# Graph attention over gathered rows: scores one block in front of the products in two layers, TensorE's second waits left out, late ring places freed by the group

## The chip, the cores and the metric

The kernel runs on one core of one Trainium2 chip. The metric is the device time of one execution in microseconds (us). The program uses five engines: TensorE (PE; its weight loads are PEld), VectorE (DVE), ScalarE (ACT), GpSimd (POOL) and SyncE (SP, which only issues DMAs here).

## What is computed

The input is `x`, 4096 nodes of 256 float32 features, and `adj`, a 4096 x 4096 int32 adjacency matrix with about 8 neighbours a row. Four graph-attention layers follow each other; each adds to `x` what it makes of the normalised rows:

```python
h = jnp.maximum(_layernorm(x, axis=-1), 0.0)
x = x + _L0_gnn_ref(h, adj, L0_gnn_W, L0_gnn_a)      # 4 heads, leaky_relu .2, softmax over neighbours, elu
...
x = x + _L1_gnn_ref(h, adj, L1_gnn_W, L1_gnn_a)      # 1 head, leaky_relu .01, h@W + att @ node
...
x = x + _L2_gnn_ref(adj, h, L2_gnn_weights, L2_gnn_biases, L2_gnn_phis)   # 4 heads, leaky_relu .2
...
x = x + _L3_gnn_ref(h, adj, L3_gnn_Wq, ...)          # 4 heads, scores q.k / 8, softmax over neighbours
```

In each layer a node's new row is a weighted sum of its neighbours' rows; the weights are a softmax over the node's neighbours. The four layers are called l=0 to l=3 below; the change's "layers two and three" are l=1 and l=2.

## The kernel before

**Lists in place of the matrix.** The function `scan` reads `adj` in 128 loads of 512 KB, turns each row into a list of neighbours, and while it reads already fetches the first six neighbours of every node for l=0 (tiles `s_g`, line L1030 of GpSimd, sums on TensorE at L630). The nodes are then put in order of their degree. `late` does the rest of l=0: 93 more fetches, in groups of up to two blocks of 128 nodes (`LATE`), into a large tile `s_ring`, products at L1237, and the rows for l=1 are scattered to a table in device memory (L1047).

**A layer.** `layer(1)`, `layer(2)` and `layer(3)` each work through 32 blocks of 128 nodes in the order 0, 30, 1, 29, ..., 17, 14, 16, 15, 31 (`ORDER`). A block has as many ring slots as its highest degree (most have 8 or 9, block 31 has 3). For each block the steps are:

- *fetch* (`fill`, L1030): GpSimd fetches one slot's 128 rows from the layer's table with an indirect DMA. The ring `s_ring` has 64 slots in l=1, 69 in l=2 and fewer, wider ones in l=3; a fetch into a used slot waits until the block that had it is done.
- *score* (`scores`): `s_e` from the fetched rows, on ScalarE in l=1 (L1507, L1508, exp at L1550, beside a check of the lists at L1564 and L1568 on VectorE), on VectorE in l=2 (L1510 to L1553, exp on ScalarE at L1556).
- *weights* (`weigh`): sum and reciprocal (L1582, L1583), shares (L1584), the node's own row (L1595, `s_me`), then VectorE scales the fetched rows in place (L1610) and TensorE sums them by products with an identity matrix: `x` itself (L1590), the scaled rows (L1617), the own row (L1623), all into `s_acc`.
- *settle* (`settle`, `normed`): VectorE reduces `s_acc` into `x` (L1644) and takes mean and variance (L955, L957); ScalarE works out scale and shift (`s_y`, L960 to L967); one step later it makes the normalised row `s_h` (L970).
- *norm* and *flip* (`turned`): TensorE transposes `s_h` (L980), ScalarE copies it out as `s_ht` (L982).
- *product* (`advance`, `times`, L1019 the bias, L1023 the weights) and *third*: the next layer's row. In l=1 it is one product of 264 columns, copied out (L1663 or L1665) and written by SP to the table of l=2 (L1667). In l=2 it is a product of 512 columns (k and v) and one of 256 (q), copied out at L1683 and L1687, multiplied and reduced (L1690, L1694), squared on ScalarE (L1697), and written by SP to the table of l=3 (L1685).

**What sets the order.** In l=1 and l=2 the order of instructions on PE, DVE, ACT and SP is the one in which the program issues them, and the loop of `layer` is written for that. For block number i of the order it fetches ahead (`fill(i)`, up to four blocks), then runs norm and product of older blocks, score and weights of block i, then settle, flip and third of older blocks. How far each stage lags behind is set by the five numbers S, N, F, Q, T, which shrink over the last blocks:

```python
S = 1 if left < 5 else 2
N = 2 if left < 4 else 3
Q = 2 if left < 2 else 3 if left < 4 else 4 if left < 6 else 5
F, T = max(N, Q - 1), Q + 1
...
p = self.scores(l, b, self.rows[b], g)
...
sums[b] = self.weigh(l, b, vs.pop(b) if l == 3 else self.rows[b][:, 0:D], g, p)
```

A layer's fetches can begin only when the table that the layer before writes is complete.

Of the kernel before, what the change touches and what calls it, by code (L numbers as in the profile page):

```python
# [75 lines left out]
AHEAD = 4  # L76

# [3 lines left out]
class Sparse:  # L81
# [500 lines left out]
    def early(self, j):  # L582


        nc, pool = self.nc, self.pool
        E, H = EARLY, 4
        two = self.keep[:, 2 * j : 2 * j + 2, :]
        g = pool.tile([P, 2, E, W], F32, name=f"s_g_{j}", tag="g", bufs=4)
        for u in range(2):
            for k in range(E):  # L590
                self.fetched = self.in_turn(
                    self.fetch(g[:, u, k, :], self.tab[0], self.ids[:, 2 * j + u, k : k + 1])
                )
        yield
        most, src, tot = (two[:, :, 2 * D + k * H : 2 * D + (k + 1) * H] for k in range(3))
        e = pool.tile([P, 2, E + 1, H], F32, name=f"s_ee_{j}", tag="ee", bufs=2)
        nc.vector.tensor_tensor(e[:, :, E, :], most, src, ALU.add)
        nc.vector.tensor_tensor(
            e[:, :, :E, :], g[:, :, :, D : D + H],
            src.unsqueeze(2).to_broadcast([P, 2, E, H]), ALU.add,  # L600
        )
        nc.vector.scalar_tensor_tensor(e, e, 0.2, e, ALU.mult, ALU.max)
        by_head = e.rearrange("p u k h -> p u h k")
        nc.vector.tensor_reduce(most, by_head, AX.X, ALU.max)
        nc.vector.tensor_tensor(
            by_head, by_head, most.unsqueeze(3).to_broadcast([P, 2, H, E + 1]), ALU.subtract
        )
        p = self.pe.tile([P, 2, E + 1, H], F32, name=f"s_pe_{j}", tag="p", bufs=1)
        nc.scalar.activation(p, e, AF.Exp)
        yield  # L610
        nc.vector.tensor_reduce(tot, p.rearrange("p u k h -> p u h k"), AX.X, ALU.add)
        me = pool.tile([P, 2, D], F32, name=f"s_mee_{j}", tag="mee", bufs=2)
        nc.vector.tensor_tensor(
            me.rearrange("p u (h d) -> p u h d", h=H),
            two[:, :, D : 2 * D].rearrange("p u (h d) -> p u h d", h=H),
            p[:, :, E, :].unsqueeze(3).to_broadcast([P, 2, H, D // H]), ALU.mult,
        )
        for u in range(2):
            yield
            v = g[:, u, :, 0:D].rearrange("p k (h d) -> p k h d", h=H)  # L620
            nc.vector.tensor_tensor(  # L621
                v, v, p[:, u, 0:E, :].unsqueeze(3).to_broadcast([P, E, H, D // H]), ALU.mult
            )
        yield
        acc = self.pp.tile([P, IB], F32, name=f"s_ae_{j}", tag="ps")
        acc = acc.rearrange("p (u d) -> p u d", u=2)
        nc.tensor.matmul(acc, lhsT=self.ident, rhs=me, start=True, stop=False)
        yield
        for k in range(E):
            nc.tensor.matmul(  # L630
                acc, lhsT=self.ident, rhs=g[:, :, k, 0:D], start=False, stop=(k == E - 1)
            )
            yield
        nc.scalar.copy(two[:, :, D : 2 * D], acc)
        yield
# [252 lines left out]
    def more_scores(self, l, mine, ge, e):  # L888
# [4 lines left out]
        if l < 3:  # L893
            nc.tensor.matmul(
                ps[:, 0:H], lhsT=self.to_edge, rhs=mine[:, D + H : D + 2 * H], start=True,
                stop=True,
            )
            nc.vector.tensor_tensor(s, ge[:, D : D + H], ps[:, 0:H], ALU.add)
        else:
            nc.tensor.matmul(ps[:, 0:D], lhsT=self.to_edge, rhs=mine[:, 0:D], start=True, stop=True)  # L900
            nc.vector.tensor_tensor(ge[:, 0:D], ge[:, 0:D], ps[:, 0:D], ALU.mult)
            nc.vector.tensor_reduce(
                s, ge[:, 0:D].rearrange("p (h d) -> p h d", h=H), AX.X, ALU.add
            )
# [9 lines left out]
        self.give(self.got)  # L914
# [12 lines left out]
        self.give(self.got)  # L927

    def more_rows(self, l, p, ge):
# [12 lines left out]
        self.give(self.got)  # L942
# [3 lines left out]
        nc.vector.tensor_tensor(v, v, s.unsqueeze(2).to_broadcast([P, H, D // H]), ALU.mult)  # L946
# [4 lines left out]
    def normed(self, pool, xt, name):  # L951
# [7 lines left out]
        log, root, less, minus, r, at = (y[:, k : k + 1] for k in range(6))  # L959
        act(log, mv[:, 1:2], AF.Ln, bias=self.eps)  # L960
# [8 lines left out]
        h = pool.tile([P, D], F32, name=f"s_h_{name}", tag="h", bufs=2)  # L969
# [3 lines left out]
    def turned(self, pool, h, name):  # L973
        nc = self.nc
        ht = pool.tile([P, KC, P], F32, name=f"s_ht_{name}", tag="ht", bufs=3)
        pt = self.bank(f"s_pht_{name}")
        self.wrote, k = [], self.groups is not None and self.got
        self.spot = pt[:, KC * P :], k
        for c in range(KC):
            self.writes(nc.tensor.transpose(pt[:, ts(c, P)], h[:, ts(c, P)], self.ident))  # L980
        yield None
        self.read_by = nc.scalar.copy(  # L982
            ht, pt[:, : KC * P].rearrange("p (c r) -> p c r", c=KC)
        ).ins
        self.give(k)
        yield ht

    def bank(self, name):
# [5 lines left out]
        self.got = k  # L994
# [20 lines left out]
    def times(self, ht, w, width, name, bias=None, ps=None):  # L1015
# [11 lines left out]
        return ps[:, :width]  # L1027

# [28 lines left out]
    def layers(self):  # L1057
        tc, nc, nt = self.tc, self.nc, self.nt
        with ExitStack() as ctx:
# [19 lines left out]
            self.past, self.took_x, self.seen = [], {}, []  # L1079
# [23 lines left out]
    def late(self):  # L1103
# [5 lines left out]
        todo, held, at = list(range(len(LATE))), {}, 0  # L1109
# [34 lines left out]
        def fill(i):  # L1144
            nonlocal at
            deliver()
            while todo and todo[0] <= i + 4:
# [4 lines left out]
                j = todo.pop(0)  # L1152
                for u, b in enumerate(LATE[j]):
                    for k in range(K):
                        last[j] = take(
                            ring[:, s + u * K + k, :], self.tab[0],
                            self.near[:, b, EARLY + k : EARLY + k + 1],
                        )
                last.setdefault(j, last.get(j - 1))
# [36 lines left out]
        def weigh(i):  # L1196
# [29 lines left out]
            g = gathered(i)  # L1226
            for u in range(m):
                for k0 in range(0, K, AT_ONCE):
                    k1 = min(k0 + AT_ONCE, K)
                    v = by_heads(g[:, u, k0:k1, 0:D])  # L1230
                    nc.vector.tensor_tensor(
# [3 lines left out]
                    )  # L1235
            for k in range(K):
                nc.tensor.matmul(  # L1237
                    acc, lhsT=self.ident, rhs=g[:, :, k, 0:D], start=False, stop=(k + 1 == K)
                )
            sums[i] = acc  # L1240

# [68 lines left out]
    def layer(self, l):  # L1310
# [8 lines left out]
        past = self.past  # L1319
# [9 lines left out]
        def fill(i):  # L1329
            nonlocal at  # L1330
            while todo and nt - len(todo) <= i + AHEAD:
# [20 lines left out]
                for k in range(K):  # L1352
                    at_k = self.near[:, j, k : k + 1]
                    g = self.fetch(ring[:, s + k, :], self.tab[l], at_k).ins
                    next_in_line(g)
                    if k == 0:
# [8 lines left out]
                    for some, _ in ends:  # L1365
                        for m in some:
                            self.tc.declare_no_dep(g, m, reason="its block's last is waited for")
# [9 lines left out]
                if more:  # L1377
                    next_in_line(self.fetch(ring[:, s + KEPT, :], self.tab[l], self.far).ins)
                held[j] = (s, s + room)
                at = s + room if K else at  # L1380

        sums, behind, turning, flipped, rows = {}, {}, {}, {}, {}
# [18 lines left out]

        def room(k):
# [4 lines left out]
        def norm(d):  # L1407
            if l < 3:
                room(1)
                turning[d] = self.turned(self.pool, next(behind.pop(d)), f"{l + 1}_{d}")  # L1410
                next(turning[d])
                when["turn", d] = now, self.wrote
# [33 lines left out]
        stages = {"settle": settle, "norm": norm, "flip": flip, "product": product, "third": third}  # L1446
# [6 lines left out]

        for i in range(nt):
            now = i
            left = nt - 1 - i
            if l == 3:
                S = 1 if left < 3 else 2
                N = F = Q = S + 1
                T = N  # L1460
            else:
                S = 1 if left < 5 else 2
                N = 2 if left < 4 else 3
                Q = 2 if left < 2 else 3 if left < 4 else 4 if left < 6 else 5
                F, T = max(N, Q - 1), Q + 1
# [4 lines left out]
            upto("norm", i - N)  # L1470
            upto("product", i - Q)
            g = ring[:, held[b][0] : held[b][1], :]
            p = self.scores(l, b, self.rows[b], g)
            if l == 3:
                upto("third", i - T)
            sums[b] = self.weigh(l, b, vs.pop(b) if l == 3 else self.rows[b][:, 0:D], g, p)
            start, end = held.pop(b)
            past.append((start * wide, end * wide, self.read))
            if l < 3:
                signals[i] = self.read[1]  # L1480
            upto("settle", i - S)
            if l < 3:
                upto("flip", i - F)
                upto("third", i - T)
# [4 lines left out]
        upto("settle", nt - 1)  # L1489
        upto("norm", nt - 1)  # L1490
# [4 lines left out]
    def scores(self, l, b, mine, g):  # L1495
# [29 lines left out]
        else:  # L1525
# [3 lines left out]
            for k0 in range(0, G, AT_ONCE):  # L1529
                m = min(AT_ONCE, G - k0)  # L1530
                kq = g[:, k0 : k0 + m, 0:D]
                nc.vector.tensor_tensor(  # L1532
                    kq, kq, q.unsqueeze(1).to_broadcast([P, m, D]), ALU.mult
                )
                nc.vector.tensor_reduce(  # L1535
# [10 lines left out]
        p = self.shares[:, ts(self.turns % 2, TOPK * H)].rearrange("p (k h) -> p k h", h=H)  # L1546
        if l == 1:
# [23 lines left out]
    def weigh(self, l, b, me, g, made):  # L1571
# [15 lines left out]
        self.turns += 1  # L1587
# [11 lines left out]
        if more:  # L1599
            rows = self.more_rows(l, p, g[:, KEPT, :])  # L1600
            some.append(
                nc.tensor.matmul(
                    acc[:, 0, :], lhsT=self.to_row, rhs=rows, start=False, stop=False
                ).ins
            )
        step = 2 if b in ORDER[-2:] else AT_ONCE
        for k0 in range(0, G, step):
            m = min(step, G - k0)
            v = g[:, k0 : k0 + m, v0 : v0 + D].rearrange("p k (h d) -> p k h d", h=H)
            nc.vector.tensor_tensor(  # L1610
                v, v, p[:, k0 : k0 + m, :].unsqueeze(3).to_broadcast([P, m, H, D // H]), ALU.mult
            )
            k = k0
            while k < k0 + m:
                n = min(2, k0 + m - k) if some else 1
                some.append(
                    nc.tensor.matmul(  # L1617
                        acc[:, 0:n, :], lhsT=self.ident, rhs=g[:, k : k + n, v0 : v0 + D],
                        start=False, stop=False,
                    ).ins  # L1620
# [9 lines left out]
    def settle(self, l, b, acc, made):  # L1630
# [5 lines left out]
        if l == 3:  # L1636
            tag = ("out", "kv")[ORDER.index(b) % 2]
# [12 lines left out]
    def advance(self, l, b, ht, made):  # L1650
# [5 lines left out]
        if l == 2:  # L1656
            short = b in ORDER[-2:]
            ps = self.times(ht, self.we2, W, name, None if short else self.be2)
            of_row = self.got
# [8 lines left out]
        else:  # L1668
            ps = self.times(ht, self.wkv, 2 * D, f"kv{name}")
            of_kv = self.got  # L1670
# [5 lines left out]
            else:  # L1676
                ps_q = self.times(ht, self.wq, D, f"q{name}")
                of_q = self.got
# [597 lines left out]
```

## Time and profile before

| | |
|---|---|
| seven runs, us | 1671.3, 1674.87, 1671.38, 1674.92, 1670.75, 1671.05, 1676.24 |
| median | 1671.38 us |
| the profiled execution | 1675.34 us, of which its span is 1673.6 us |
| mean granted TensorE clock | 0.831 |
| PE busy | 1076.5 us (64%), 3179 instructions |
| PEld busy | 586.0 us (35%) |
| DVE busy | 1109.5 us (66%), 2651 instructions |
| ACT busy | 535.8 us (32%), 1754 instructions |
| POOL busy | 1141.6 us (68%), 1241 instructions |

The profile is of one execution. Times are us from the start of its span. A row of a timeline gives the start, the duration, the engine, the line of the kernel, the operation and the tiles (out <- in), a count where several like instructions follow each other, and in brackets how long the engine was idle before it and what released it. A group gives busy time and mean duration, and then the idle time ahead of its instructions. The stages lie about like this: scan to 350, late 366 to 545, l=1's fetches 545 to 883, l=2's 909 to 1247, l=3's from 1282 on.

### The profile page before, as it was taken

The page shows a single profiled execution, that of the slowest core. Times are in us where ns is not written, and L with a number is a line of the kernel's source. Part 1 is how long each engine was busy: PE and PEld are TensorE (multiplying, and loading weights), DVE is VectorE, ACT ScalarE, POOL GpSimd, SP SyncE. Part 2 cuts the span into 40 slices and gives each one's busy share as a digit, 9 for nine tenths or more (in the row PEclk, how much of TensorE's full clock was granted, in tenths as well). Part 3 has the DMA queues.
Part 4 walks back from the last instruction along what each step waited for, and adds up shares of the span by engine and source line. Part 5 has one row for each costly group of instructions (what it writes and reads, how often), then busy time and mean ns, then how long its engine had stood idle before and what let it go on. Part 6 is the DMA issues. An engine that isn't in the chain of part 4 may idle for free.

```text
span 1673.6 us, 14552 instructions
## 1 busy us (share of the span) xinstructions
PE 1076.5 (64%) x3179; PEld 586.0 (35%) x3179; DVE 1109.5 (66%) x2651; ACT 535.8 (32%) x1754; POOL 1141.6 (68%) x1241
## 2 busy tenths in 40 slices
PE   5858878605776357777775477778794455545465
PEld 4523333203443134444343234444452222322232
DVE  5669899816885254455552456676774797888777
ACT  6966665003344023333343023333342000000000
POOL 1167777767774777777772777777762777777775
PEclk9969989857897578898897689999997677777878
DMA  7899999466552344444452435444542776767674
GB/s 265 287 395 394 359 395 337 140 217 175 154 167 68 110 119 128 131 132 131 132 138 65 109 108 145 137 134 134 146 130 89 209 220 206 215 202 213 202 209 143
DMA packets 125910, 309.11 MB, mean 185 GB/s; under 512 B 35028, under 2 KB 53463, under 8 KB 125816
## 3 DMA queue, kind: packets, MB, share of 16 engines
q0 software_dynamic: 66832, 203.64, 41.7%
q1 hardware_dynamic: 58984, 104.46, 17.6%
q8 instruction: 29, 0.48, 0.1%
q14 instruction: 65, 0.53, 0.1%
HBM read 273.00 MB, written 35.00 MB: 184 GB/s over the span
## 4 chain that ended last, share of the span: by engine, by line
POOL 26%; DMA 23%; DVE 19%; issue 16%; ACT 9%; PE 6%; DVEq 0%; POOLq 0%; SPq 0%; ACTq 0%
POOL s_ring L1030 21%; DMA s_ring<-s_tab,s_near 12%; DMA s_raw<-in_adj_dram 9%; DVE s_ring L1610 5%; ACT s_low L277 2%; POOL s_placed L721 2%; POOL s_g L1030 2%; DVE s_ring L1532 1%; DVE s_e L1535 1%; PE s_acc L1237 1%; PE s_bank L1023 1%; PE s_ps_t L1023 1%; DVE s_rx L1644 1%; DVE s_me L1595 1%; POOL out_dram L1047 1%
## 5 line engine op out<-in xcount | busy, mean ns | idle before, releaser
L1030 POOL DMA_INDIRECT s_ring<-s_tab,s_near x900 | 854.3, 949 | 339.9 <-issue 263.0
L1617 PE MATMUL s_acc<-s_ring,s_ident 128*128 128x512 f32 (+1 forms) x1002 | 454.4, 610 | 278.4 <-DVE s_ring L1610 278.3
L1617 PEld LDWEIGHTS s_acc<-s_ring,s_ident 128*128 128x128 f32 x1002 | 221.1, 228 | 489.8 <-DVE s_ring L1610 309.1
L1030 POOL DMA_INDIRECT s_g<-s_tab,s_keep x192 | 183.2, 954 | 131.6 <-DMA s_raw<-in_adj_dram 67.6
L1610 DVE TENSOR_TENSOR s_ring<-s_ring,s_shares 128x2048 f32<-128x2048 f32 (+1 forms) x153 | 233.0, 1554 | 0.0
L277 ACT ACTIVATE s_low<-s_raw 128x1024 fp8e4<-128x1024 int32 x128 | 135.1, 1055 | 64.1 <-DMA s_raw<-in_adj_dram 62.1
L1556 ACT ACTIVATE s_shares<-s_e 128x40 f32<-128x40 f32 (+7 forms) x64 | 13.1, 205 | 331.6 <-DVE s_e L1553 331.6
L520 PE MATMUL s_pt<-s_low,s_mark_True 128*128 128x512 fp8e4 x256 | 83.6, 407 | 53.6 <-DVE s_cand L532 47.2
L1532 DVE TENSOR_TENSOR s_ring<-s_ring,s_shares 128x2048 f32<-128x2048 f32 (+7 forms) x47 | 78.8, 1676 | 56.2 <-DMA s_ring<-s_tab,s_near 38.2
L960 ACT ACTIVATE s_y<-s_mv,s_eps 128x1 f32<-128x1 f32 x64 | 18.8, 294 | 276.6 <-DVE s_mv L957 250.5
L532 DVE MAX8 s_cand<-s_pt 128x8 f32<-128x256 f32 x256 | 93.4, 420 | 13.8 <-PE s_pt L530 13.8
L1564 DVE TENSOR_SCALAR s_eq<-s_ring,s_own_f 128x207 bf16<-128x207 f32 (+12 forms) x32 | 12.4, 388 | 131.9 <-DMA s_ring<-s_tab,s_near 131.7
L630 PE MATMUL s_ae<-s_g,s_ident 128*128 128x512 f32 x192 | 94.3, 622 | 3.4 <-DVE s_g L621 3.4
L1535 DVE TENSOR_REDUCE s_e<-s_ring 128x32 f32<-128x2048 f32 (+7 forms) x47 | 78.9, 1679 | 1.6
L1023 PE MATMUL s_bank<-s_wkv,s_ht 128*128 128x512 f32 x128 | 66.3, 644 | 3.6 <-ACT s_ht L982 3.6
L1023 PE MATMUL s_ps<-s_we_l,s_ht 128*128 128x264 f32 x128 | 45.9, 514 | 23.9 <-ACT s_ht L1271 23.9
L520 PEld LDWEIGHTS <-s_mark_True 128*128 128x128 bf16 x256 | 23.4, 101 | 105.1 <-issue 54.8
L1590 PE MATMUL s_acc<-s_rx,s_ident 128*128 128x256 f32 x192 | 59.9, 395 | 0.0
L1623 PE MATMUL s_acc<-s_me,s_ident 128*128 128x256 f32 x192 | 57.1, 379 | 0.0
L1268 PE MATMUL s_pht<-s_ident,s_rx 128*128 128x128 f32 x64 | 13.8, 325 | 65.6 <-ACT s_rx L1261 57.9
L621 DVE TENSOR_TENSOR s_g<-s_g,s_pe 128x1536 f32<-128x1536 f32 x32 | 55.5, 1740 | 0.0
L922 PE MATMUL s_bank<-s_to,s_to_row 128*128 128x32 f32 (+1 forms) x6 | 1.8, 394 | 81.1 <-DVE s_to L916 81.1
(286 smaller groups left out, 1842.0 us busy)
## 6 DMA issues: line engine op xcount, KB each, us to landing
s_raw<-in_adj_dram SPq DMA_DIRECT2D x128, 512.0 KB, 9.8
s_ring<-s_tab,s_near POOLq DMA_INDIRECT x900, 3.0
s_rx<-s_placed SPq DMA_DIRECT2D x32, 262.0 KB, 3.8
s_tab<-s_kv SPq DMA_DIRECT2D x32, 256.0 KB, 2.3
s_tab<-s_rx SPq DMA_DIRECT2D x32, 132.0 KB, 2.0
s_keep<-in_x_dram SPq DMA_DIRECT2D x8, 512.0 KB, 9.4
s_vself<-s_tab SPq DMA_DIRECT2D x32, 128.0 KB, 3.4
s_tab<-s_keep SPq DMA_DIRECT2D x7, 528.0 KB, 3.2
```

The source lines that it names most:

```text
L277: nc.scalar.activation(low[r][:, quarter(q)], raw.pop(q), AF.Copy, saturate=False, accum_out=self.sums[:, r, h : h + 1],)
L520: nc.tensor.matmul(pt, lhsT=self.mark[k], rhs=lo[:, k * PAIR + g * IB : k * PAIR + (g + 1) * IB], start=(k == 0), stop=False,)
L532: nc.vector.max(out=cand[:, g * (IB // CH) + k, :], in_=pt[:, ts(k, CH)])
L630: nc.tensor.matmul(acc, lhsT=self.ident, rhs=g[:, :, k, 0:D], start=False, stop=(k == E - 1))
L1023: self.writes(self.nc.tensor.matmul(ps[:, :width], lhsT=ht[:, c, :], rhs=w[:, c, :], start=(c == 0 and bias is None), stop=(c == KC - 1),))
L1030: return self.nc.gpsimd.indirect_dma_start(out=out, out_offset=None, in_=table[:, :], in_offset=bass.IndirectOffsetOnAxis(ap=idx, axis=0),)
L1532: nc.vector.tensor_tensor(kq, kq, q.unsqueeze(1).to_broadcast([P, m, D]), ALU.mult)
L1535: nc.vector.tensor_reduce(e[:, k0 : k0 + m, :], kq.rearrange("p k (h d) -> p k h d", h=4), AX.X, ALU.add)
L1590: self.took_x[b] = nc.tensor.matmul(acc[:, 1, :], lhsT=self.ident, rhs=self.x[b], start=True, stop=False)
L1610: nc.vector.tensor_tensor(v, v, p[:, k0 : k0 + m, :].unsqueeze(3).to_broadcast([P, m, H, D // H]), ALU.mult)
L1617: nc.tensor.matmul(acc[:, 0:n, :], lhsT=self.ident, rhs=g[:, k : k + n, v0 : v0 + D], start=False, stop=False,).ins
L1623: last = nc.tensor.matmul(acc[:, 0, :], lhsT=self.ident, rhs=mev, start=False, stop=True).ins
```

## The change

It has three parts.

1. *TensorE's second waits.* The products that sum fetched rows (L630, L1237, L1617) follow VectorE's scaling of the same rows, which has itself waited for the fetches. A new helper `behind` declares that a product need not wait for the fetches too. A second helper, `covered`, does the same for VectorE's scaling and for fetches against the earlier products on reused ring slots (`ever`).
2. *Late ring places.* In `late`, the first fetch of a group that takes over ring slots waits for the last product of the group that had them; the other rows' own waits for single products are left out.
3. *Scores in front.* In l=1 and l=2, block i+1's score is issued ahead of block i's weights, except for the last two turns (`left` of 1 or 0), the ScalarE part of the norm becomes a stage `curve` of its own, and the lags come from a table `LAGS`. The tile `s_h` has three buffers instead of two, and l=3's output tile takes them over. l=3's loop keeps its order.

The core of the diff:

```diff
+LAGS = [
+    (1, 1, 2, 2, 2), (1, 1, 2, 2, 2), (1, 1, 2, 2, 3), (1, 1, 3, 3, 3), (1, 2, 3, 3, 4),
+    (2, 2, 3, 3, 4), (2, 2, 4, 4, 5), (2, 3, 4, 5, 6),
+]
...
@@ normed
         y = pool.tile([P, 6], F32, name=f"s_y_{name}", tag="y1", bufs=3)
         log, root, less, minus, r, at = (y[:, k : k + 1] for k in range(6))
+        yield None
         act(log, mv[:, 1:2], AF.Ln, bias=self.eps)
...
-        h = pool.tile([P, D], F32, name=f"s_h_{name}", tag="h", bufs=2)
+        h = pool.tile([P, D], F32, name=f"s_h_{name}", tag="h", bufs=3)
...
+    def covered(self, g, start, size):
+
+        for a, b, some in self.ever:
+            if a < start + size and start < b:
+                for o in some:
+                    self.tc.declare_no_dep(g, o, reason="its block's last is waited for")
+
+    def behind(self, got, product):
+
+        for f in got:
+            self.tc.declare_no_dep(product.ins, f, reason="VectorE's products come in between")
+        return product
...
@@ late, fill
+                ends = [e for a, b, e in past if a < high and low < b]
...
+                        if u == k == 0:
+                            for _, end in ends:
+                                self.tc.add_manual_dep(
+                                    g, end.name,
...
+                                    reason="the group's slots are free",
+                                )
+                        self.covered(g, (s + u * K + k) * W, W)
...
@@ layer
+        def curve(c):
+            if l < 3:
+                next(behind[c])
+                bent[c] = next(behind.pop(c))
...
+            else:
+                S, Y, N, F, Q = LAGS[min(left, len(LAGS) - 1)]
+                score(i)
+                if left > 1:
+                    score(i + 1)
+                upto("norm", i - N)
+                upto("product", i - Q)
+                sums[b] = self.weigh(l, b, self.rows[b][:, 0:D], block(b), scored.pop(b))
+                signals[i] = self.read[1]
             start, end = held.pop(b)
             past.append((start * wide, end * wide, self.read))
-            if l < 3:
-                signals[i] = self.read[1]
             upto("settle", i - S)
             if l < 3:
+                upto("curve", i - Y)
                 upto("flip", i - F)
-                upto("third", i - T)
+                upto("third", i - Q - 1)
...
@@ weigh
-                    nc.tensor.matmul(
+                    self.behind(self.got.get((l, b), ()), nc.tensor.matmul(
                         acc[:, 0:n, :], lhsT=self.ident, rhs=g[:, k : k + n, v0 : v0 + D],
                         start=False, stop=False,
-                    ).ins
+                    )).ins
```

## The prediction

> **What bounds the kernel now.** I read the page's chain and groups first, then what GpSimd waited for, then the timelines of the two places where GpSimd stands still.
>
> The page, sections 4 and 5 (columns of a group: busy us, mean ns | idle before it, releaser):
>
> ```profile
> POOL 26%; DMA 23%; DVE 19%; issue 16%; ACT 9%; PE 6%; DVEq 0%; POOLq 0%; SPq 0%; ACTq 0%
> ...
> L1030 POOL DMA_INDIRECT s_ring<-s_tab,s_near x900 | 854.3, 949 | 339.9 <-issue 263.0
> ```
>
> One fetch of 128 neighbour rows is 0.95 us on GpSimd. The timeline of GpSimd has it start every 1.25 us (878.09 after 876.84), with 0.30 us between two that wait for nothing shown. So 270 fetches of a layer take 270 x 1.25 = 337.5 us, and l=1 runs from 545.48 to 882.8, l=2 from 908.98 to 1247.2: GpSimd sets the pace and never waits for a ring slot there. What it does wait for is in the list of its waits (total us, times, longest):
>
> ```profile
> POOL s_ring L1030 <- issue: 263.9, 774, 26.2
> ...
> POOL s_ring L1030 <- PE s_bank L1722: 35.3, 1, 35.3
> ```
>
> The 26.2 us stand ahead of l=2's first fetch (908.98), the 35.3 us ahead of l=3's (1282.49; L1722 is named, but the wait is for the last DMA into l=3's table). They are **drains**: the last rows land, their blocks go through scores, weights, sum, norm, product and table, and only then can the next layer fetch. Whatever the change does between two drains is hidden under 1.25 us a fetch as long as GpSimd gets its slots; what it does in a drain counts fully.
>
> VectorE in the drain of l=2 (start us, us, instruction, [idle before <- releaser]), and in that of l=1:
>
> ```profile
> 1242.70 0.43 DVE L955 BATCH_NORM_STATS2 s_st<-s_rx 128x6 f32<-128x256 f32 x1
> ...
> 1246.30 0.69 DVE L1683 TENSOR_TENSOR s_kv<-s_bank,s_bqkv 128x512 f32<-128x512 f32 x1 [1.13 <-PE s_acc L1623]
> ...
> 1251.74 0.15 DVE L1510 TENSOR_TENSOR s_e<-s_rx 128x4 f32<-128x4 f32 x1
> ...
> 1254.03 2.48 DVE L1610 TENSOR_TENSOR s_ring<-s_ring,s_shares 128x512 f32<-128x512 f32 x4
> ...
> 1261.36 0.17 DVE L1582 TENSOR_REDUCE s_t<-s_shares 128x4 f32<-128x16 f32 x1 [2.80 <-ACT s_shares L1556]
> ```
>
> ```profile
> 881.03 0.32 DVE L1564 TENSOR_SCALAR s_eq<-s_ring,s_own_f 128x184 bf16<-128x184 f32 x1 [2.31 <-DMA s_ring<-s_tab,s_near]
> ...
> 884.65 2.47 DVE L1610 TENSOR_TENSOR s_ring<-s_ring,s_shares 128x512 f32<-128x512 f32 x4
> 887.05 0.68 DVE L1644 TENSOR_REDUCE s_rx<-s_acc 128x256 f32<-128x512 f32 x1
> ...
> 892.68 0.16 DVE L1522 SCALAR_TENSOR_TENSOR s_e<-s_e 128x4 f32<-128x4 f32 x1 [3.79 <-ACT s_e L1508]
> ```
>
> In l=1, VectorE has nothing left when block 15's rows land (2.31 us idle). In l=2 its rows land about 1245.4 (the last of its fetches is issued at 1242.5, and a fetch lands 2.9 us after its start), and its score waits until 1251.74 behind older blocks' work.
>
> **Part 1: TensorE's second waits.** By the order of instructions, 492 waits go and no matmul. In the trace such a wait is 51 ns on TensorE's weight queue, 25 us in all. But an eight-slot block's products take 3.54 us with four of them (1242.12 to the start of L1623 at 1245.66) and 3.44 in block 15 of l=1, where they stand coarser (885.88 to 889.32): 0.1 us a block by the pace, 0.2 by 4 x 51 ns. In steady state TensorE waits for GpSimd's rows and it is worth 0; about ten blocks stand in the drains of late, l=1, l=2 and at the end of l=3, half of them on the chain: 0 to -2 us, I take **-0.5**, nearest to the pace.
>
> **Part 2: late ring places.** 27 of late's 93 fetches reuse a slot. Now the group's first fetch waits for the last product of the group it replaces, not each row for its own. All GpSimd's gaps in late up to 514 are 0.30, so no row waits there now. A later release costs at most a group's products (3.5 us), and a slot comes round after some 60 x 1.25 = 75 us, while in l=1 block 16's slots are held 23 us (first fetch 859.3, last product 881.9) and late's groups wait no longer. I take **0** (0 to +3.5). Cover gone, it would be 3.5 us on GpSimd.
>
> **Part 3: the score in front, the norm's ScalarE part as a step of its own, new lags.** GpSimd's and SP's order of issue is unchanged, so fetches, sends and table writes keep their places; only PE, DVE and ACT are reordered, in l=1 and l=2. Block i+1's score now stands ahead of block i's weights on VectorE, so **weights of i cannot start before the rows of i+1 have landed**. What queues behind that: scale, products, settling of older blocks. Between drains a block's rows come every 8 x 1.25 = 10 us, and slots are free one block later: the 23 us for which a slot is held become 33, against 80 us (64 or 69 slots of 1.25) until it comes round. I take 0 there. In a drain it means that a block's weights, which were finished in the idle time before the last rows, are now still to do when they land.
>
> l=1, steps from rows of before (weights without scale 0.74, scale of 8 slots 2.28, in four pieces 2.40, settle with statistics 1.29, products of a block 3.54 + last 0.44):
> - rows of 15 land 881.03; e_15 no longer stands behind h_14 and ht_14 on ScalarE (1.5 us earlier), score done about 881.9;
> - now weights and scale of 16 (before: 874.41 to 877.4): ring_16 882.9 to 885.1, settle of 14 to 886.4;
> - ring_15 887.15 to 889.55 (before 884.65 to 887.05): +2.5;
> - TensorE: sum of 16 to 889.0, products of 17 and 14 (1.73 each), sum of 15 to 897.0 (before 889.8), product of 16, sum of 31 to 901.2 (before 897.5): +3.7;
> - y_31 started at 900.07, 1.2 us after its statistics (898.9), behind ht_15; with statistics at 902.5 it starts at once: **+2.5**, and h, transposes, product, row and DMA follow as before.
>
> l=2 (score 0.95, weights 1.03, scale 2.28, k/v/q group 1.85):
> - rows of 16 land 1235.4; score to 1236.4; k/v/q of 19 and 12 to 1240.1; weights and scale of 14 to 1243.6, settle of 17 to 1244.9 (before: 1235.1);
> - score of 15 at 1245.4 instead of 1251.74, to 1246.35; k/v/q of 18 to 1248.2; weights and scale of 16 to 1251.45 (before 1242.0), settle of 14 to 1252.7;
> - TensorE: sum of 16 to 1255.35; the first half (1.72) of product 17 to 1257.4, and its k/v/q, which now stand ahead of weights of 15, to 1259.4;
> - weights and ring_15 to 1262.9 (before 1256.42): +6.5; settle and h of 16, exp of 31 at 1266.7 (before 1261.14): +5.5; sum of 31 at 1272 to 1274 (before 1267.98): +4 to +6.1; then as before.
>
> I take **+6**. Bounds: without TensorE's chain VectorE alone would bring ring_15 to 1260.3, and the 2.80 us idle at 1261.36 could take some back: +3. If product 14 too stays on the chain (2.58): +8.5. For l=1: 0 (the wait of 1.2 and 1.5 us of e_15 taken in) to +3.7.
>
> **Sum:** -0.5 + 0 + 2.5 + 6 = +8.0. The profiled execution, 1675.34 us (span 1673.6 and 1.74 around it), would become 1683.3. It lies 4 us above the median, in the upper of two groups of the seven runs (1670.75 to 1671.38 and 1674.87 to 1676.24); against the median 1671.38 the sum is **1679.4**.
>
> On the clock: product 31 of l=1 takes 2.13 us at a granted clock of 0.50 (903 to 906) against 1.16 for product 15; product 16's first half in l=2 3.67 at 0.57 against 1.88. I keep these. The Trainium skill (TensorE: Matmul & The Clock Gate, Part 1: The HAM clock gate) says the clock halves after about an idle window of 3.4 us and comes back after as long a busy one; that speaks for the change, which packs the drain's matmuls closer. By it both products would be fast, some 2.8 us less, and the sum an estimate of 1676.6. The rows fit it only in part: the gaps ahead of the 3.67 are 1.49 and 0.46 us.
>
> **Rivals.**
> - **The drains shorten (other side, faster).** Mechanism: ScalarE's and VectorE's round trips overlap. Place: l=1's e_15 (1.5 us late behind h_14), l=2's 2.80 us idle ahead of L1582. For it: both idles are real, and scores are ready earlier. Against it: the last block's score is still behind y_16 and h_16. It decides once VectorE is through weights of 16 before block 15 lands; I have it 6 us behind. Price -1.5 - 2.8 - 0.5: 1666.6.
> - **All is hidden.** VectorE's idle in l=2's drain (1.13, 0.98, 0.57 and 2.80, 5.5 in all) takes the deferred block up, l=1's slack of 1.2 and 1.5 the other: -0.5, 1670.9. Against it: TensorE's sums follow each other without a gap from 1234.77 to 1246.2, so the block cannot be caught up there.
> - **Slots come late in steady state.** The deferred weights hold a block's slots 10 us longer; if GpSimd waited even 0.3 us at half of 60 blocks, +9 more: 1688. Against it: no gap above 0.30 in both layers, and 80 us a turn of the ring.
> - **The waits were worth more than the pace shows:** 51 ns each in all drains, -2 instead of -0.5: 1677.9, on the forecast's side.
>
> **How the numbers follow.** About 0.2% (3.3 us) is what a measurement here can tell from no change: faster is below 1668.0, slower above 1674.7. Drains longer: 0.63 (1675 to 1686, by the bounds of l=1, l=2). Slots late: 0.07 (to 1690 and over). Hidden: 0.13 (1668 to 1674.7). Drains shorter: 0.17 (1665 to 1668). So faster 0.17, same 0.13, slower 0.70. The range leaves out some of the shorter drains and of the late slots: 1667 to 1690; the forecast's own is 1675 to 1686.
>
> **What would show it.** GpSimd's wait ahead of l=2's first fetch 28 to 29 us instead of 26.19, ahead of l=3's 41 instead of 35.27; no GpSimd gap above 0.30 elsewhere in l=1, l=2 and late; block 16's scale after block 15's score in both drains; L1617's products 0.1 us a block shorter. Wrong: if the two waits fall, the order of TensorE's products was misjudged; if they stand and the time moves, it came from late, l=3 or GpSimd's pace.

## The result, and the profile after

The changed kernel takes 1684.38 us (median of 15 runs, 1680.26 to 1689.14); the kernel before, over 38 runs, 1672.42 us. The ratio is 1.0071, 95% interval 1.0063 to 1.0080: 11.9 us slower, where +8.0 was forecast and 1667 to 1690 us was the range.

The profiled execution takes 1680.75 us, of which 1678.8 is its span. The list of GpSimd's waits of the kernel after (total us, times, longest) has the two rows that matter:

```profile
POOL s_ring L1053 <- issue: 273.4, 796, 29.0
...
POOL s_ring L1053 <- PE s_bank L1785: 42.5, 1, 42.5
```

L1053 is the fetch (L1030 before), L1785 stands where L1722 did. The wait ahead of l=2's first fetch went from 26.19 to 29.01 us (+2.8), the one ahead of l=3's from 35.27 to 42.49 (+7.2). Between the drains nothing moved: l=1's fetches take 337.3 us from first to last in both profiles, l=2's 338.2 and 338.3, l=3 with its end 391.1 and 390.8, and no other gap of GpSimd in l=1 and l=2 is above 0.31 us.

The two drains make +10.0 of the 11.9 us. The profiled pair differs by less, 5.4 us, because l=1 happened to begin at 540.95 in it and at 545.48 in the one before; over the six profiles taken where the kernel before needs 1672 to 1676 us this start lies between 540.95 and 545.48 in no order of the versions. Late's first fetch already varies as much (360.92 to 365.83), so most of the difference comes from the scan, which all share.

VectorE in the drain of l=2, kernel before: the scale of block 16 and the last k and v (the score of block 15 stands at 1251.74, between them):

```profile
1239.79 2.28 DVE L1610 TENSOR_TENSOR s_ring<-s_ring,s_shares 128x2048 f32<-128x2048 f32 x1
...
1278.93 0.69 DVE L1683 TENSOR_TENSOR s_kv<-s_bank,s_bqkv 128x512 f32<-128x512 f32 x1 [2.56 <-PE s_bank L1023]
```

Kernel after:

```profile
1245.22 0.19 DVE L1572 TENSOR_TENSOR s_e<-s_ring,s_rx 128x32 f32<-128x32 f32 x1
...
1248.08 0.69 DVE L1746 TENSOR_TENSOR s_kv<-s_bank,s_bqkv 128x512 f32<-128x512 f32 x1 [1.92 <-PE s_acc L1686]
...
1250.94 2.28 DVE L1672 TENSOR_TENSOR s_ring<-s_ring,s_shares 128x2048 f32<-128x2048 f32 x1
...
1257.51 0.69 DVE L1746 TENSOR_TENSOR s_kv<-s_bank,s_bqkv 128x512 f32<-128x512 f32 x1 [3.00 <-PE s_acc L1686]
...
1262.92 2.47 DVE L1672 TENSOR_TENSOR s_ring<-s_ring,s_shares 128x512 f32<-128x512 f32 x4
...
1269.33 0.17 DVE L1645 TENSOR_REDUCE s_t<-s_shares 128x4 f32<-128x16 f32 x1 [1.88 <-ACT s_shares L1619]
...
1284.48 0.69 DVE L1746 TENSOR_TENSOR s_kv<-s_bank,s_bqkv 128x512 f32<-128x512 f32 x1 [2.56 <-PE s_bank L1033]
```

The first row is the score of block 15, about 1.5 us after its rows land (its last fetch starts at 1240.87, and landing takes 2.9 us as in the prediction), where it waited about 6 us before; the 1250.94 row is the scale of block 16, which before was done ahead of it. To compare drains, count from the end of the layer's last fetch (1247.22 before, 1245.56 after): the scale of 16 starts at +5.4 instead of -7.4, that of 15 at +17.4 instead of +6.8, that of 31 at +24.7 instead of +15.1, and the last k and v at +38.9 instead of +31.7.

In l=1's drain block 16's scale, at 875.16 before, now stands behind block 15's score (876.43 is the list check of 15, 878.06 the scale of 16):

```profile
876.43 0.32 DVE L1627 TENSOR_SCALAR s_eq<-s_ring,s_own_f 128x184 bf16<-128x184 f32 x1 [4.51 <-DMA s_ring<-s_tab,s_near]
...
878.06 2.28 DVE L1672 TENSOR_TENSOR s_ring<-s_ring,s_shares 128x2048 f32<-128x2048 f32 x1
```

TensorE's sums of 16, 15 and 31 follow each other with only older blocks' products in between, two behind the first sum and one behind the second:

```profile
880.39 3.71 PE L1680 MATMUL s_acc<-s_ring,s_ident 128*128 128x256 f32 x10 [0.60 <-DVE s_ring L1672]
883.93 0.59 PE L1686 MATMUL s_acc<-s_me,s_ident 128*128 128x256 f32 x2
...
888.47 3.60 PE L1680 MATMUL s_acc<-s_ring,s_ident 128*128 128x256 f32 x10
891.90 0.59 PE L1686 MATMUL s_acc<-s_me,s_ident 128*128 128x256 f32 x2
...
896.00 0.59 PE L1686 MATMUL s_acc<-s_me,s_ident 128*128 128x256 f32 x2
```

The statistics of block 31 end 19.8 us after the last fetch; worked out were 19.7 (902.5 less 882.8).

### The profile page after: what moved, and what is told of

Read it like the earlier page. It is cut to its first block, busy times and chain, and to the rows that moved or that the text cites. A ratio compares the mean times of both kernels' runs of the same rounds, so it can differ in the third digit from the quotient of the medians.

```text
span 1678.8 us, 14043 instructions
## 1 busy us (share of the span) xinstructions
PE 1079.1 (64%) x3179; PEld 589.5 (35%) x3179; DVE 1103.5 (66%) x2651; ACT 539.1 (32%) x1754; POOL 1141.3 (68%) x1241
## 4 chain that ended last, share of the span: by engine, by line
POOL 30%; DMA 22%; issue 19%; DVE 17%; PE 6%; ACT 6%; DVEq 0%; SPq 0%; POOLq 0%; ACTq 0%
POOL s_ring L1053 26%; DMA s_raw<-in_adj_dram 10%; DMA s_ring<-s_tab,s_near 10%; DVE s_ring L1672 3%; PE s_acc L1680 2%; ACT s_low L281 2%; POOL s_placed L726 2%; DVE s_ring L1593 2%; POOL s_g L1053 2%; DVE s_e L1597 1%; PE s_bank L1033 1%; POOL out_dram L1070 1%; PE s_ps_t L1033 1%; DVE s_ring L1269 1%; PE s_acc L1277 1%
## 5 line engine op out<-in xcount | busy, mean ns | idle before, releaser
L1053 POOL DMA_INDIRECT s_ring<-s_tab,s_near x900 | 854.7, 950 | 349.7 <-issue 272.8
L1680 PE MATMUL s_acc<-s_ring,s_ident 128*128 128x512 f32 (+1 forms) x1002 | 472.7, 630 | 309.2 <-DVE s_ring L1672 309.1
L1680 PEld LDWEIGHTS s_acc<-s_ring,s_ident 128*128 128x128 f32 x1002 | 226.1, 234 | 530.1 <-DVE s_ring L1672 343.7
L1053 POOL DMA_INDIRECT s_g<-s_tab,s_keep x192 | 182.7, 952 | 128.5 <-DMA s_raw<-in_adj_dram 66.2
L1672 DVE TENSOR_TENSOR s_ring<-s_ring,s_shares 128x2048 f32<-128x2048 f32 (+1 forms) x153 | 233.0, 1554 | 0.0
L1593 DVE TENSOR_TENSOR s_ring<-s_ring,s_shares 128x2048 f32<-128x2048 f32 (+7 forms) x47 | 78.8, 1676 | 55.7 <-DMA s_ring<-s_tab,s_near 36.0
L1572 DVE TENSOR_TENSOR s_e<-s_ring,s_rx 128x36 f32<-128x36 f32 (+12 forms) x32 | 6.3, 195 | 109.7 <-DMA s_ring<-s_tab,s_near 79.5
L1568 ACT ACTIVATE s_e<-s_ring,s_rx 128x9 f32<-128x9 f32 (+12 forms) x32 | 9.9, 308 | 200.1 <-DMA s_ring<-s_tab,s_near 190.1
L1033 PE MATMUL s_bank<-s_wkv,s_ht 128*128 128x512 f32 x128 | 61.0, 599 | 4.4 <-ACT s_ht L992 4.4
```

The source lines that it names most:

```text
L1033: self.writes(self.nc.tensor.matmul(ps[:, :width], lhsT=ht[:, c, :], rhs=w[:, c, :], start=(c == 0 and bias is None), stop=(c == KC - 1),))
L1053: return self.nc.gpsimd.indirect_dma_start(out=out, out_offset=None, in_=table[:, :], in_offset=bass.IndirectOffsetOnAxis(ap=idx, axis=0),)
L1593: scaled = nc.vector.tensor_tensor(kq, kq, q.unsqueeze(1).to_broadcast([P, m, D]), ALU.mult)
L1672: scaled = nc.vector.tensor_tensor(v, v, p[:, k0 : k0 + m, :].unsqueeze(3).to_broadcast([P, m, H, D // H]), ALU.mult)
L1680: self.behind(self.got.get((l, b), ()), nc.tensor.matmul(acc[:, 0:n, :], lhsT=self.ident, rhs=g[:, k : k + n, v0 : v0 + D], start=False, s ...
```

## The experiments

**Theory.** The score in front makes block i's weights wait for the rows of i+1; in each drain one block's weights, sum, settling and product are then still to do, and that is the loss. **Rivals:** the new lags and the norm's own ScalarE step make it; the waits and places carry the 2 us beyond the drains; within the drain, a wait for the turn's last sum that the prediction left out is on the chain.

Twelve runs were made in three sets. The second set ran where the kernel before takes 1675.88 us (25 runs), and carries the verdicts. The first and third met a chip on which the kernel before takes 2007.09 and 1984.42 us; what they can say is told after it.

### Without the score in front

```diff
                 score(i)
-                if left > 1:
-                    score(i + 1)
                 upto("norm", i - N)
```

> The changed kernel without the score in front once more, since the first set met a chip on which the kernel before takes 2007 us and engines stand idle for microseconds with nothing shown that they wait for. Where the kernel before takes about 1672 us: theory (the score in front lengthens the drains) waits of 25 to 27 and 34 to 37 us, time -1 to +2 us against before; rival (the new lags and the split norm do it) 29 and 42 us, +10 to +12. Where it takes about 2007 us: -21 us again, as the first set had.

Measured: 1671.46 us, ratio 0.9977 (0.9965 to 0.9990): -3.9 us by the ratio, -4.4 by the medians. GpSimd's waits:

```profile
POOL s_ring L1053 <- issue: 262.8, 779, 23.5
...
POOL s_ring L1053 <- PE s_bank L1783: 35.3, 1, 35.3
```

Both fall back; l=1's is even 2.7 us shorter than before, below the 25 to 27 that were expected. So the score in front is the loss, and the rest of the third part is a gain: this version is 3.0 us below the old loop with parts 1 and 2 in the same set (1674.45, below). VectorE in l=1's drain shows where part of it comes from:

```profile
878.14 0.32 DVE L1625 TENSOR_SCALAR s_eq<-s_ring,s_own_f 128x184 bf16<-128x184 f32 x1 [3.77 <-DMA s_ring<-s_tab,s_near]
879.63 0.16 DVE L1644 RECIPROCAL s_t<-s_t 128x1 f32<-128x1 f32 x1 [0.52 <-ACT s_e L1611]
```

From block 15's rows to its weights are 1.5 us. In the kernel before they are 2.9 (881.03 to 883.91), because ScalarE makes h and ht of 14 ahead of 15's score:

```profile
881.06 0.61 ACT L970 ACTIVATE s_h<-s_rx,s_y 128x256 f32<-128x256 f32 x1
882.20 0.37 ACT L982 COPY s_ht<-s_bank 128x256 f32<-128x256 f32 x1 [0.53 <-PE s_bank L980]
882.50 0.31 ACT L1507 ACTIVATE s_e<-s_ring,s_rx 128x8 f32<-128x8 f32 x1
```

With the new lags h of 14 is made in the 3.77 us of waiting for rows. That is 1.4 of the 2.7 us.

### The score in front only up to the fifth turn from the end

```diff
-                if left > 1:
+                if left > 3:
                     score(i + 1)
```

> The score in front only up to the fifth turn from the end, once more. At about 1672 us for the kernel before: theory waits of 26 to 27 and 35 to 38 us, time 0 to +3 us; rival (lags) +10 to +12. At about 2007 us: -27 us again.

Measured: 1685.64 us, ratio 1.0065 (1.0046 to 1.0084); waits of 30.16 and 42.79 us. The theory's numbers failed: as slow as the whole change, although the weights of 14 and 16 no longer wait for the next rows. Only those of 17 still do, and the timeline of VectorE in l=2 shows what follows:

```profile
1232.15 2.28 DVE L1672 TENSOR_TENSOR s_ring<-s_ring,s_shares 128x2048 f32<-128x2048 f32 x1
...
1236.88 0.66 DVE L1746 TENSOR_TENSOR s_kv<-s_bank,s_bqkv 128x512 f32<-128x512 f32 x1
...
1238.70 0.69 DVE L1746 TENSOR_TENSOR s_kv<-s_bank,s_bqkv 128x512 f32<-128x512 f32 x1
...
1240.64 0.69 DVE L1746 TENSOR_TENSOR s_kv<-s_bank,s_bqkv 128x512 f32<-128x512 f32 x1
...
1244.18 2.61 DVE L1672 TENSOR_TENSOR s_ring<-s_ring,s_shares 128x2048 f32<-128x2048 f32 x2
...
1248.26 0.19 DVE L1572 TENSOR_TENSOR s_e<-s_ring,s_rx 128x32 f32<-128x32 f32 x1
```

The last fetch ends at 1250.0. The scale of 17 (1232.15) is already late, and between it and the scale of 14 (1244.18) stand two settlings and three k/v/q groups that the shrinking lags call up. The score of 16 (1248.26) is thereby some 10 us after its rows. A window says the same: from 1222 to 1247 (core's us, then busy us of PE, PEld, DVE, ACT, POOL, the clock, the DMA share, GB/s)

```profile
1222.00:1247.00 25.00, 23.23 (x78) 13.91 (x77) 22.83 (x50) 12.35 (x50) 18.91 (x21) 1.00 0.57 162
```

TensorE and VectorE are both over 90% busy, so in l=2 there is little room to work off a block that was put off before.

In l=1 this is not the reason: from 850 to 875 TensorE is busy for 18.64 and VectorE for 16.34 of 25 us, and the wait behind it, 30.16 us, is still the longest of the second set. There the rows show something else:

```profile
865.64 6.55 PE L1680 MATMUL s_acc<-s_ring,s_ident 128*128 128x256 f32 x10 [5.18 <-DVE s_ring L1672]
...
879.03 0.17 DVE L1583 SCALAR_TENSOR_TENSOR s_e<-s_e 128x9 f32<-128x9 f32 x1 [4.11 <-ACT s_e L1569]
```

TensorE stands idle for 5.18 us until block 17's late scale, and the sum of 17 then takes 6.55 us at a granted clock of 0.59 (865.6 to 872.6). Behind it ScalarE makes scale, shift and h of two blocks (873.15 to 878.06) before the score of 16, for which VectorE waits 4.11 us. No run took any of this away, so why a block that is put off stays put off is read from this profile, not shown. That the score must move back well before the lags shrink is a guess from it; the run meant to show it (front only while more than ten turns are left) met the other chip.

### The old loop, with waits left out and late places

```diff
+            elif l in (1, 2):
+                S = 1 if left < 5 else 2
+                N = 2 if left < 4 else 3
+                Q = 2 if left < 2 else 3 if left < 4 else 4 if left < 6 else 5
...
+                upto("norm", i - N)
+                upto("product", i - Q)
+                score(i)
```

> Parts 1 and 2 alone, once more. At about 1672 us for the kernel before: theory -0.5 us (0 to -2) and waits of 26 and 35 us; rival (these parts carry the 2 us by which the measured +12 is above the drains' 10) +2 us. At about 2007 us: -17 us again.

Measured: 1674.45 us, ratio 0.9997 (0.9984 to 1.0009): -0.5 us by the ratio (-2.7 to +1.5), -1.4 by the medians; waits 25.79 and 34.89. Parts 1 and 2 are worth nothing that can be told from zero, and do not add the 2 us beyond the drains.

### Reads wait for their own product

In the last seven turns, `third` no longer replaces the wait for a product by the one for the turn's last sum:

```diff
                 next(rows.pop(d), None)
-                if step < now:
+                if step < now and left > 6:
                     for i in self.reads:
                         told_by(i, wrote, step)
```

> The changed kernel, but in a layer's last seven turns what reads a product (k, v, q or the row of the next layer) waits for that product and no longer for the last sum of the turn in which it was issued. Theory (in l=2's drain the k and v of 18 and of 13 stand behind the sums of 14 and 16, 1.92 and 3.00 us, which the prediction left out): the wait ahead of l=3's first fetch falls from 42.5 to 39.5 to 40.5, that of l=2 stays at 28 to 29, time +9 to +10 us against before instead of +12. Rival (these waits are idle time of an engine that is not on the chain): 42.5 stays, +12.

Measured: 1683.97 us, ratio 1.0050 (1.0031 to 1.0068), +8.4 us by the ratio; GpSimd's waits:

```profile
POOL s_ring L1053 <- issue: 273.0, 793, 29.3
...
POOL s_ring L1053 <- PE s_bank L1785: 39.0, 1, 39.0
```

VectorE takes k and v of 18 right behind the score of 15:

```profile
1246.71 0.19 DVE L1572 TENSOR_TENSOR s_e<-s_ring,s_rx 128x32 f32<-128x32 f32 x1 [0.82 <-DMA s_ring<-s_tab,s_near]
...
1247.55 0.68 DVE L1746 TENSOR_TENSOR s_kv<-s_bank,s_bqkv 128x512 f32<-128x512 f32 x1
```

l=2's drain gives back 3.5 us of its 7.2, l=1's none, as the theory had it and a little more. The two waits on sums are on the chain; k and v of 18 now start 0.8 us before the last fetch ends instead of 2.5 after it.

### The sets on the other chip

There the fetches keep their pace (0.95 us each, 1.25 from start to start), but every engine stands idle at times for 3 to 10 us and more, for which the trace gives "issue" (nothing shown that it waits for) or "remote" (a releaser that it does not name; GpSimd alone has 19 such waits, 87.1 us, in the run below). The group of sums on the page of the old loop with parts 1 and 2 there (busy us, mean ns | idle before, releaser):

```profile
L1693 PE MATMUL s_acc<-s_ring,s_ident 128*128 128x512 f32 (+1 forms) x1002 | 460.7, 613 | 290.1 <-issue 157.6
```

In the kernel before, the same group's idle time was VectorE's scale almost alone (278.3 of 278.4). GpSimd's waits ahead of l=2 and l=3 are 53 to 69 and 80 to 94 us there, in all eight versions; a drain's order is lost in them. What was expected and measured:

Without the score in front (edit as above):

> The changed kernel without the score in front (score of i just ahead of norm, product and weights of i); the new lags, the norm's ScalarE step, the left-out waits and the late places stay. Theory (the score in front lengthens the drains): GpSimd's wait ahead of l=2's first fetch falls from 29.0 back to 25 to 27 us, that ahead of l=3's from 42.5 to 34 to 37; time 0 to -1 us against the kernel before, plus 2 at most. Rival (the new lags and the split norm do it): the waits stay at 29 and 42, time +10 to +12 us.

1986.08 us, ratio 0.9896 (0.9870 to 0.9922).

> The changed kernel with the score in front only up to the fifth turn from the end: the scores of blocks 16, 15 and 31 stand right ahead of their own weights again. Theory: weights of 14 and 16 no longer wait for the rows of 16 and 15, so most of the drains' growth goes: waits of 26 to 27 and 35 to 38 us, time +0 to +3 us against before. Rival (lags): 29 and 42, +10 to +12. A third (the score in front costs something over the whole of a layer): time stays at +10 though the waits fall.

1980.19 us, ratio 0.9873 (0.9847 to 0.9899): with the score in front up to the fifth turn from the end, the reverse of the other chip's 1.0065.

> Parts 1 and 2 alone: the loop of the kernel before in l=1 and l=2, with TensorE's second waits left out and late's places freed by the group. Theory: -0.5 us, within -2 and 0; the waits of GpSimd 26.2 and 35.3 less 0.2 to 0.6. Rival (the 2 us that the measured +12 is above the 10 of the two drains come from these parts): +2 us. Other rival (the waits matter more): -2 us or below.

1988.36 us, ratio 0.9915 (0.9875 to 0.9954).

The places alone, as the run before it, but `behind` does nothing:

```diff
         for f in got:
-            self.tc.declare_no_dep(product.ins, f, reason="VectorE's products come in between")
+            pass
```

> Part 2 alone: as the run before this one, but TensorE's products wait for the fetches again. Theory: 0 us (within 0.7), and against parts 1 and 2 together +0.5. Rival: +2 us if a group's first fetch in late now waits longer; then GpSimd shows gaps above 0.3 us in late before its tail.

2001.46 us, ratio 0.9983 (0.9953 to 1.0014). Beside the run before it, TensorE's 492 waits left out look worth 13 us there; but the two intervals overlap, so it is not shown.

In the third set all four kernels leave these waits out. The score in front while more than ten turns are left (`if left > 10:`):

> The changed kernel with the score in front only while more than ten turns are left. Theory after the run that stopped at the fifth turn from the end (one block's weights once put off are a backlog on VectorE and TensorE, which the last turns, with their shrinking lags, have no room to work off; earlier turns have): waits of 23 to 25 and 35 to 36 us as without any score in front, time -2 to -5 us against before. Rival (the score in front costs something in every turn, or through what it leaves in the buffers): waits of 29 and 42 again, +10 to +12.

1984.68 us, ratio 1.0006 (0.9978 to 1.0033).

The old loop with `if left > 1: score(i + 1)` behind `score(i)`:

> The score in front (except in the last two turns) with the lags of the kernel before and without the norm's ScalarE step; waits left out and late places stay. Theory (the score in front alone makes the loss, whatever the lags): waits of 28 to 31 and 40 to 46 us, +8 to +15 us against before. Rival (the loss needs the new lags, which shrink from 6 to 2 in the last turns): 25 to 27 and 35 to 37, within 2 us of before.

1986.48 us, ratio 1.0014 (0.9985 to 1.0043).

Neither score in front nor the wait for the turn's last sum (both edits above):

> No score in front, and in the last seven turns what reads a product waits for that product and not for the turn's last sum. The run without the score in front had waits of 23.5 and 35.3 us and -4 us against before; three waits of VectorE for sums (1.88, 1.88 and 2.50 us) are left in l=2's drain. Theory (they are on the chain, as in the changed kernel, where they were worth 3.5): 23 to 23.5 and 32 to 34 us, time -5 to -8 us. Rival (without the score in front VectorE has that time to spare): 35, -4 us.

1980.86 us, ratio 0.9982 (0.9950 to 1.0015).

The old loop with the wait for the product itself:

> The loop of the kernel before in l=1 and l=2, waits left out, late places, and in the last seven turns the wait for the product itself. It tells what the new lags and the norm's ScalarE step are worth beside the one before it in this set. Theory: l=1 as with the old loop, 25.8 us; l=2 33 to 34 instead of 34.9; -2 us against before, so the new lags are worth some 3 to 4 us. Rival (with that wait gone, old and new lags come out alike): both within 1 us of each other.

1974.04 us, ratio 0.9959 (0.9929 to 0.9989).

These four decide nothing: their numbers were expected for drains of 23 to 46 us. The kernel before itself moved from 2007 to 1984 between the two sets, more than any two of them differ by. So it stays open whether a score in front that ends earlier is free, whether it costs as much with the old lags, and whether the wait for the own product adds to the gain of the version without the score in front. That version is the fastest that was measured against the others: 1671.46 us where the kernel before has 1675.88 and parts 1 and 2 alone 1674.45.

## Why the prediction was right

- **What bounds the kernel:** right. Both layers between their drains took what they took before to 0.1 us; all that could be placed lies in the two waits of GpSimd that were named.
- **Part 1, -0.5:** -0.5 by the ratio, not to be told from 0. But the step behind it was wrong. The trace has 55 of the 51-ns waits on L1680's weight queue where L1617 had 414, and an eight-slot block still takes 3.54 us (880.39 to 883.93) or 3.43 (888.47 to 891.90), much the same two values as before. Behind idle time it is 3.54 in both kernels (0.60 us of it at 880.39). Without, it is mostly 3.4, but 3.54 in the prediction's own block at 1242.12. So the 0.1 us were not the waits.
- **Part 2, 0:** right; the only gaps of GpSimd in late above 0.31 us are in its tail, as before.
- **Part 3, l=1, +2.5:** +2.8; block 31's statistics came 19.8 us after the last fetch, 19.7 by the steps.
- **Part 3, l=2, +6:** +7.2, the term that was mis-sized, and by two errors that partly cancel. The steps had k/v/q of 18 right behind block 15's score and of 13 at once; in fact they wait for the sums of 14 and 16 (1.92 and 3.00 us), because in this loop a read of a product waits for the turn's last sum, and with the weights deferred that sum is late. Ring_15 was worked out to end 15.7 us after the last fetch and ended at 19.8. The run with own products has 3.5 us of the wait back. By the steps alone those 4.1 us would have made +10. At the other end TensorE was faster than the 3.67 and "then as before" that were kept: product 16's first half took 1.98 us at a granted clock of 1.00 (1270 to 1275), and k, v and q of 15 took 2.85 us (1277.70 to 1280.55) instead of 4.49 (1270.50 to 1274.99, where the clock was 0.66). That the miss is only 1.2 us is in part luck.
- **The clock:** by the Trainium skill (TensorE: Matmul & The Clock Gate, Part 1: The HAM clock gate) the prediction's estimate was 2.8 us less for two products, packed closer. One came (3.67 to 1.98); the other, product 31 of l=1, stayed at 2.13 us at a granted clock of 0.54 (901 to 904), behind gaps of 2.04 and 0.46 us. Neither gap is as long as the page's idle window of about 3.4 us, so there the measurement departs from the page. Half of the estimate came.
- **Rivals:** shorter drains did not come, since the scale of 16 in l=2 began 5.4 us after the last fetch, not before block 15's rows. "All is hidden" failed, but not on TensorE alone as argued: its sums of 14 and 16 wait 1.44 and 1.28 us for VectorE's scales (1243.48 and 1253.28), while VectorE waits 1.92 and 3.00 us for the same sums. Slots came in time.
- **The sum:** +8.0 against 11.9 (10.5 to 13.4). The drains make 10.0 of it in one execution of each kernel. In the four runs of the second set the change of the two waits and that of the time (by the ratio) lie up to 1.6 us apart, in both directions, so the last 2 us are hardly more than such readings scatter; no run placed them.

## What to carry to other kernels

Issuing a step early to fill an engine's round trip puts the step behind it off until the early one's input has come: between the drains that was free here, as the buffers lasted, but where a stage must drain the deferred step has to be counted (here +2.8 and +7.2 us). Turning the order back four turns ahead of the end gave nothing back here, so the block was still put off at the end. And when an order is changed, look at what waits were merged into "the last of the turn": what was harmless with the last one early is on the chain when it is late.

## What the runs showed of the hardware

The same kernel took 1672 and 1676 us in two sets and 1984 and 2007 in two others, on another chip, with the same pace of indirect fetches (1.25 us) and the same durations of single instructions (the scale of fetched rows 1554 ns in the mean in both), but with idle stretches on all engines that the trace ascribes to nothing or to "remote", such as 9.97 us of TensorE from 1405.7 on in the old loop's run. What causes them was not found. There a version can even come out the other way round (0.9873 against 1.0065 for the same kernel), so a verdict on drains of a few us needs the kernel before on the same chip, and a profile of it that shows no such stretches.
